# Opening blocks of a two-step top-p attention: the first probe of block 0 (in step 1 also of block 3) moved to VectorE, block 0's mask moved ahead of block 1's probes, and step 1's exponentials put in another order

## The chip, the cores and the metric

The kernel runs on one core of one Trainium2 chip. Times are device microseconds of that core. Most figures are a median of several executions; a figure "in the profile" is from the one execution that the hardware profiler recorded. All executions reported here count as fast ones: on a single core that only means that none lay more than 1.5% above the fastest of the same kernel.

Engines are named as in the profile: PE is TensorE (PEld its loading of weights), DVE is VectorE, ACT is ScalarE, POOL is GpSimd. The granted clock is the share of TensorE's full clock that the profile shows as granted. TensorE is called warm where its operations take their usual time and cold where they take longer: four transposes take 0.60 to 0.66 us warm and some 1.1 us cold in these profiles.

"VectorE's lock" is a name for something that the profiles show of GpSimd. In the first profiles of the two kernels, from 1550 to 3300 us, 232 GpSimd operations started 0.1 us or more after one of VectorE's operations of 4.5 us on 128 x 4096 elements (probes and masks) had started and before it ended: all 232 ended only after it. Where none of these VectorE operations was under way, no GpSimd operation on one column took more than 0.77 us. An operation that ends late in this way is called held.

## The reference, cut to what matters

The program has two layers. The change concerns the second one, which runs two steps of attention over 4096 nodes with the exact top-p ("nucleus") set of each row kept:

```python
def _top_p_attention(X, W1, W2, W3):
    q = X @ W1.T @ W2.T
    k = X @ W3.T
    logits = q @ k.T / TAU
    probs = jax.nn.softmax(logits, axis=-1)
    idx = jnp.argsort(-probs, axis=-1)
    sp = jnp.take_along_axis(probs, idx, axis=-1)
    cs = jnp.cumsum(sp, axis=-1)
    keep_sorted = cs - sp < TOP_P            # 0.9
    ...
    A = probs * mask
    return A / jnp.maximum(A.sum(-1, keepdims=True), 1e-12)

for n in range(STEPS):                       # 2
    A = _top_p_attention(Xa, W1, W2, W3)
    Xf = R @ Xf
    Xa = A @ Xa
    Z = Z + Xf @ U1[n].T + Xa @ U2[n].T
# then X + Z, layer norm over the 256 features
```

## The kernel before

Rows are handled in 32 blocks of 128. Nothing is sorted. For each block the kernel computes the exponentials `e` (128 x 4096, float32), then closes in on the threshold: a "probe" is a sum of all the elements at or below a guess, and some arithmetic on one column turns it into a better guess. After the last probe, what is below the guess is kept in `big`, its largest elements are drawn out ("candidates"), the exact threshold is read off their running sum, and a mask zeroes what is below. TensorE then transposes the masked block and multiplies it with X.

Who does what: TensorE the logits, transposes and products; ScalarE the exponentials, the first probe and the copies out of PSUM; GpSimd the column arithmetic that makes each guess; VectorE the later probes, the candidates and the mask. Step 0 has three probes; step 1, whose first guess is better, skips the second. In the cut below, lines that only allocate or slice are left out.

```python
def exponentials(r, c):                       # 4 of these a block, ScalarE
    nc.scalar.activation(ev[:, :, c, :], r.pm[c], AF.Exp, bias=r.nm, accum_out=...)

def first_probe(r, i):                        # 4 of these a block, ScalarE: sums of Relu and Sign of c1 - e
    nc.scalar.activation(void, r.e[:, ts(h, N // 2)], (AF.Relu, AF.Sign)[i], bias=r.c1, scale=-1.0,
                         accum_out=r.sums[:, h, 2 + i:3 + i])

def lowered(c, y, more):                      # GpSimd: the next guess
    t = col("lowered", 6)
    pool.tensor_tensor(t, inv_e, y, ALU.pow)
    pool.tensor_scalar(t, t, c, more, ALU.mult, ALU.mult)
    return t

def first_step(r):                            # GpSimd, on single columns
    ...                                       # sums, z, L from the four partial sums; r.y1 = fall(r, L)
    if not last:
        r.c2 = lowered(r.c1, r.y1, 1.0)
        pool.tensor_tensor(r.yy, r.y1, r.y1, ALU.mult)
    pool.tensor_tensor(r.up, r.z, mone, ALU.pow)
    pool.tensor_scalar(r.up, r.up, r.sg, ...)
    if last:
        ...
        r.c3 = lowered(r.c1, r.y1, r.up)

def second_probe(r):                          # VectorE, then 17 small operations of GpSimd; step 0 only
    nc.vector.scalar_tensor_tensor(junk, r.e, r.c2, r.e, ALU.is_le, ALU.mult, accum_out=L)
    ...
    r.c3 = lowered(r.c2, y, up)

def third_probe(r):                           # VectorE
    nc.vector.scalar_tensor_tensor(big, r.e, r.c3, r.e, ALU.is_le, ALU.mult, accum_out=r.L)

def masked(r):                                # VectorE
    nc.vector.scalar_tensor_tensor(r.e, r.e, r.t, r.e, ALU.is_ge, ALU.mult, accum_out=kept)

# one step; AHEAD is 4
for b in range(AHEAD):
    ...                                       # 4 x (logits, exponentials) of block b
    for i in range(4):
        first_probe(r, i)
    if b < 2:
        first_step(r)
    if b == 0:
        second_probe(r)
        third_probe(r)
for b in range(NB):
    if b + 1 < NB:
        second_probe(blocks[b + 1])
    candidates(r, found)
    if b + 2 < NB:
        first_step(blocks[b + 2])
    if b + 1 < NB:
        third_probe(blocks[b + 1])
    ...                                       # finishing of earlier blocks
    masked(r)
    attend(r, cur, blocks.get(b - 1), blocks.get(b + AHEAD))
```

`attend` holds TensorE's work on the masked block, and ScalarE's copies, exponentials and first probe of the block four ahead. The program fixes each engine's list, in the order in which it names the operations, and in the profiles the operations behind one that waits come after it. That is why order alone can be worth time here.

Of the kernel before, what the change touches and what calls it, by code (L numbers as in the profile page):

```python
# [20 lines left out]
ALU = mybir.AluOpType  # L21
# [20 lines left out]
AHEAD = 4  # L42
# [5 lines left out]
def gat_then_top_p_diffusion(  # L48
# [562 lines left out]
    def began(n, b, kT, qT, nm, sg, thr, c1):  # L611
        r = SimpleNamespace(n=n, b=b, kT=kT, q=qT[:, ts(b, P)], nm=nm[:, b:b + 1], sg=sg[:, b:b + 1], thr=thr[:, b:b + 1],
                            c1=c1[:, b:b + 1])
        r.e = l1e.tile([P, N], F32, name="e1")
        r.sums = small.tile([P, 2, 4], F32, name="sums", bufs=6)
        return r

    def exponentials(r, c):

        ev = r.e.rearrange("p (h c n) -> p h c n", h=2, c=4)  # L620
        nc.scalar.activation(ev[:, :, c, :], r.pm[c], AF.Exp, bias=r.nm, accum_out=r.sums[:, c // 2, c % 2:c % 2 + 1])  # L621

    def first_probe(r, i):


        h, i = divmod(i, 2)
        void = l1.tile([P, N // 2], I8, name="void")
        nc.scalar.activation(void, r.e[:, ts(h, N // 2)], (AF.Relu, AF.Sign)[i], bias=r.c1, scale=-1.0,  # L628
                             accum_out=r.sums[:, h, 2 + i:3 + i])

    def fall(r, low):

        a, d = col("a"), col("d")
        pool.tensor_scalar(a, r.z, TOP_P - 1.0, low, ALU.mult, ALU.add)
        pool.tensor_scalar(d, r.z, PHI / 0.64, a, ALU.mult, ALU.add)
        pool.tensor_tensor(d, d, mone, ALU.pow)
        pool.tensor_scalar(a, a, d, r.sg, ALU.mult, ALU.mult)
        return a
# [8 lines left out]
    def first_step(r):  # L647
        s, L = r.sums, col("L")
        last = r.n + 1 == STEPS
        r.z, r.yy, r.up = col("z", 6), col("yy"), col("up")  # L650
        pool.tensor_tensor(s[:, 0], s[:, 0], s[:, 1], ALU.add)  # L651
        pool.tensor_scalar(r.z, s[:, 0, 0:1], s[:, 0, 1:2], None, ALU.add)
        pool.tensor_scalar(L, s[:, 0, 3:4], float(N), 0.5, ALU.add, ALU.mult)
        pool.tensor_scalar(L, L, r.c1, s[:, 0, 2:3], ALU.mult, ALU.subtract)
        r.y1 = fall(r, L)
        if not last:
            r.c2 = lowered(r.c1, r.y1, 1.0)
            pool.tensor_tensor(r.yy, r.y1, r.y1, ALU.mult)
        pool.tensor_tensor(r.up, r.z, mone, ALU.pow)
        pool.tensor_scalar(r.up, r.up, r.sg, 0.64 * (11.0 if last else 14.0) / PHI, ALU.mult, ALU.mult)  # L660
        if last:

            pool.tensor_scalar(r.yy, r.y1, -0.2, None, ALU.mult)
            pool.tensor_scalar(r.yy, r.y1, 0.2, r.yy, ALU.mult, ALU.max)
            pool.tensor_scalar(r.yy, r.yy, 1.0, None, ALU.add)
            pool.tensor_scalar(r.up, r.up, r.c1, r.yy, ALU.mult, ALU.add)
            r.c3 = lowered(r.c1, r.y1, r.up)

    def second_probe(r):
        if r.n + 1 == STEPS:  # L670
            return
        L = col("L")
        nc.vector.scalar_tensor_tensor(junk, r.e, r.c2, r.e, ALU.is_le, ALU.mult, accum_out=L)
        rho, y, up = col("rho"), col("y"), col("up2")
        y2 = fall(r, L)

        pool.tensor_scalar(rho, r.y1, y2, r.y1, ALU.subtract, ALU.mult)
        pool.tensor_scalar(rho, rho, 1e-7, None, ALU.max)
        pool.tensor_tensor(rho, rho, mone, ALU.pow)
        pool.tensor_scalar(rho, rho, r.yy, 0.5, ALU.mult, ALU.max)  # L680
        pool.tensor_scalar(rho, rho, 2.0, -1.0, ALU.min, ALU.add)
        pool.tensor_scalar(rho, r.yy, r.thr, rho, ALU.is_gt, ALU.mult)
        pool.tensor_scalar(y, rho, 1.0, y2, ALU.add, ALU.mult)

        pool.tensor_tensor(y2, y, y, ALU.mult)
        pool.tensor_scalar(rho, y2, 3.5, 0.3, ALU.mult, ALU.add)
        pool.tensor_scalar(y2, rho, y2, 1.0, ALU.mult, ALU.add)
        pool.tensor_scalar(up, r.up, r.c2, y2, ALU.mult, ALU.add)
        r.c3 = lowered(r.c2, y, up)

    def third_probe(r):

        r.L = col("L3")
        nc.vector.scalar_tensor_tensor(big, r.e, r.c3, r.e, ALU.is_le, ALU.mult, accum_out=r.L)  # L694

    def candidates(r, found):


        t, after, eighth = (x[:, r.b:r.b + 1] for x in found)
        seg = SEG[r.n + 1 == STEPS]  # L700
        cand = small.tile([P, max(SEG), 8], F32, name="cand", bufs=2)[:, :seg]
        best = small.tile([P, CAND], F32, name="best", bufs=2)

        cum = small.tile([P, CAND + 1], F32, name="cum", bufs=2)
        edges = [N * s // seg for s in range(seg + 1)]
        for s in range(seg):
            nc.vector.max(cand[:, s, :], big[:, edges[s]:edges[s + 1]])  # L707
        nc.vector.tensor_scalar(cum[:, :1], r.z, 1.0 - TOP_P, r.L, ALU.mult, ALU.subtract)
        nc.vector.tensor_reduce(eighth, cand[:, :, 7], AX.X, ALU.max)
        flat = cand.rearrange("p s k -> p (s k)")  # L710
        for i in range(CAND // 8):
            nc.vector.max(best[:, ts(i, 8)], flat)
            if i + 1 < CAND // 8:
                nc.vector.match_replace(flat, best[:, ts(i, 8)], flat, -1.0)
        nc.vector.tensor_tensor_scan(cum[:, 1:], best, zero.to_broadcast([P, CAND]), cum[:, :1], ALU.add, ALU.add)

        drop = small.tile([P, CAND], F32, name="drop", bufs=2)
        work = small.tile([P, CAND], F32, name="work", bufs=2)
        nc.vector.tensor_scalar(drop, cum[:, :CAND], 0.0, 3.0e38, ALU.is_ge, ALU.mult)
        nc.vector.tensor_tensor_reduce(work, drop, best, 1.0, best[:, :1], ALU.add, ALU.min, t)  # L720
        nc.vector.tensor_scalar(work, drop, -1.0, 3.0e38, ALU.mult, ALU.add)
        nc.vector.tensor_tensor_reduce(work, best, work, 1.0, -3.0e38, ALU.subtract, ALU.max, after)
        r.t = t
# [221 lines left out]
    for n in range(STEPS):  # L945
        if n == 0:
            cur = X
        else:
            cur = X
            for g in range(NB // 4):  # L950
                nc.sync.dma_start(cur[:, ts(g, 4), :], xa_d[ts(g, 4)].rearrange("b p d -> p b d"))
        kT, qT, nm, sg, thr, c1 = projections(cur, n)
        found = [table(f"found{i}") for i in range(3)]
        every = {ET.DVE, ET.PE, ET.Activation, ET.Pool}
        blocks = {}
        with tc.manual_schedule(engines=every):
            for b in range(AHEAD):
                r = blocks[b] = began(n, b, kT, qT, nm, sg, thr, c1)
                r.pm = {}
                for c in range(4):  # L960
                    r.pm[c] = logits(r.q, kT, c)
                    exponentials(r, c)
                for i in range(4):
                    first_probe(r, i)
                if b < 2:
                    first_step(r)
                if b == 0:
                    second_probe(r)
                    third_probe(r)
            for b in range(NB):  # L970
                r = blocks[b]
                if b + 1 < NB:
                    second_probe(blocks[b + 1])
                candidates(r, found)
                if b > 2:
                    finish_scale(blocks[b - 3])
                if b + 2 < NB:
                    first_step(blocks[b + 2])
                if b + 1 < NB:
                    third_probe(blocks[b + 1])  # L980
                if b > 1:
                    finish(blocks[b - 2])
                if b > 2:
                    finish_rows(blocks.pop(b - 3))
                masked(r)
                if b + AHEAD < NB:
                    blocks[b + AHEAD] = began(n, b + AHEAD, kT, qT, nm, sg, thr, c1)
                attend(r, cur, blocks.get(b - 1), blocks.get(b + AHEAD))
            r = blocks[NB - 1]
            finish(blocks[NB - 2])  # L990
            contributed(r, contribute(r))
            finish(r)
            for b in range(NB - 3, NB):
                finish_scale(blocks[b])
            for b in range(NB - 3, NB):
                finish_rows(blocks[b])
        repaired(n, kT, qT, nm, cur, found)
# [32 lines left out]
```

## Time and profile before

| | before |
|---|---|
| median of three executions | 3413.57 us (3408.16 to 3417.34) |
| span in the profile | 3405.8 us, granted clock 0.945 |
| first exponential of step 0 to the start of its last mask | 805.99 us |
| first exponential of step 1 to the end of the program | 901.48 us |
| in step 1: first exponential to TensorE's first product | 59.88 us |
| in step 1: one block on TensorE | 24.33 us |

The page's first line of figures gives the busy time of each engine in us, its share of the span and the count of its instructions:

```profile
PE 3023.5 (89%) x19243; PEld 2431.8 (71%) x19243; DVE 2616.3 (77%) x5070; ACT 2009.1 (59%) x3182; POOL 1160.3 (34%) x1804
```

These shares average over stages that are limited by different engines, so they say little on a change at two openings.

To compare executions I set the clock of each step to zero at that step's first exponential. What lies before it (the first layer, projections, the reload of X between the steps) differs by some microseconds from execution to execution and has nothing to do with the change: the first exponential of step 0 came at 1553.8 to 1565.0 us over all profiles of this study.

### The profile page before, as it was taken

How to read it: one execution, taken by the hardware profiler on the slowest of the kernel's cores; microseconds unless marked ns; L12 is line 12 of the kernel's file. 1: busy time of each engine (PE TensorE's matmuls, PEld its weight loads, DVE VectorE, ACT ScalarE, POOL GpSimd, SP SyncE). 2: the span in 40 equal slices, each digit the busy share in tenths (PEclk: the TensorE clock that was granted, in tenths of full speed). 3: DMA queues.
4: the chain of work that ended last, by engine and by line, in shares of the span. 5: the costliest groups of instructions: out<-in, count | busy, mean ns of one | idle time of the engine just before them, and what ended most of it. 6: DMA issues, size and time to landing. Idle time of an engine off the chain costs nothing. (4 is left out here: it accounts for less than half of the span.)

```text
span 3405.8 us, 52192 instructions
## 1 busy us (share of the span) xinstructions
PE 3023.5 (89%) x19243; PEld 2431.8 (71%) x19243; DVE 2616.3 (77%) x5070; ACT 2009.1 (59%) x3182; POOL 1160.3 (34%) x1804
## 2 busy tenths in 40 slices
PE   4499898898989999983999999999849999999994
PEld 3399798897968888751777777777526777777783
DVE  6589898999966555414999999997148888888864
ACT  4588787886841100046676767672367777777731
POOL 3100201102010000006776767672034656565620
PEclk7699999999999999986999999999869999999997
DMA  9726548383155555400000000000100000000000
GB/s 262 209 89 171 172 118 244 106 215 128 44 169 172 163 171 167 131 11 1 13 16 18 16 18 17 18 16 18 61 1 10 24 21 24 21 24 21 24 19 11
DMA packets 198827, 268.62 MB, mean 79 GB/s; under 512 B 14240, under 2 KB 156064, under 8 KB 198560
## 3 DMA queue, kind: packets, MB, share of 16 engines
q1 hardware_dynamic: 152272, 207.99, 18.8%
q0 software_dynamic: 16896, 33.56, 5.4%
q10 hardware_dynamic: 29392, 23.60, 2.2%
q8 instruction: 157, 2.57, 0.3%
q14 instruction: 110, 0.90, 0.1%
HBM read 226.89 MB, written 71.76 MB: 88 GB/s over the span
## 5 line engine op out<-in xcount | busy, mean ns | idle before, releaser
L800 PE MATMUL acc<-X,eT 128*128 128x256 f32 x4160 | 977.1, 381 | 8.3 <-ACT eT L794 8.3
L800 PEld LDWEIGHTS acc<-X,eT 128*128 128x128 f32 x4160 | 763.8, 191 | 95.4 <-ACT eT L794 8.8
L284 PE MATMUL acc<-ut,m 128*128 128x195 bf16 (+1 forms) x8192 | 730.3, 249 | 85.5 <-DVE m L272 49.4
L284 PEld LDWEIGHTS <-m 128*128 128x128 bf16 x8192 | 702.4, 98 | 113.4 <-DVE m L272 66.4
L265 ACT ACTIVATE g<-sr,d_big 128x1024 bf16<-128x1024 f32 x512 | 550.6, 1180 | 49.8 <-DVE m L271 39.8
L628 ACT ACTIVATE void<-e,c 128x2048 int8<-128x2048 f32 x256 | 514.6, 2010 | 1.0
L621 ACT ACTIVATE e<-mm,nm 128x1024 f32<-128x1024 f32 x256 | 286.0, 1117 | 341.9 <-PE mm L483 341.8
L425 PE MATMUL racc<-hl,ar 128*128 128x512 f32 x2048 | 470.5, 392 | 14.8 <-issue 10.4
L425 PEld LDWEIGHTS racc<-hl,ar 128*128 128x128 f32 x2048 | 385.8, 189 | 99.3 <-issue 11.3
L794 ACT COPY eT<-tp 128x512 f32<-128x512 f32 x520 | 303.8, 584 | 171.8 <-PE tp L792 171.8
L792 PEld LDWEIGHTS tp<-ident,e 128*128 128x128 f32 x2080 | 246.2, 142 | 212.8 <-issue 95.5
L792 PE MATMUL tp<-ident,e 128*128 128x128 f32 x2080 | 325.2, 280 | 51.4 <-DVE e L773 29.9
L483 PE MATMUL mm<-kT,qT 64*128 64x512 f32 x1024 | 303.8, 679 | 61.6 <-ACT e L621 50.9
L271 DVE TENSOR_TENSOR m<-g,ax 128x2048 bf16<-128x2048 bf16 x256 | 313.1, 1223 | 41.7 <-ACT g L265 38.7
L707 DVE MAX8 cand<-big 128x8 f32<-128x228 f32 (+1 forms) x1088 | 343.8, 394 | 0.0
L272 DVE TENSOR_TENSOR m<-ax,m 128x2048 bf16<-128x2048 bf16 x256 | 315.9, 1234 | 26.2 <-PE acc L284 0.5
L694 DVE SCALAR_TENSOR_TENSOR big<-e,lowered 128x4096 f32<-128x4096 f32 x64 | 286.8, 4481 | 34.0 <-POOL lowered L644 34.0
L421 DVE CAST ar<-at 128x1024 fp32r<-128x1024 bf16 x256 | 177.1, 692 | 169.5 <-PE racc L425 166.5
L728 DVE SCALAR_TENSOR_TENSOR e<-e,found 128x4096 f32<-128x4096 f32 x64 | 287.6, 4494 | 0.0
L436 ACT ACTIVATE xf<-xf,rinv 128x256 f32<-128x256 f32 x64 | 32.6, 510 | 372.3 <-DVE xf L435 370.0
L651 POOL TENSOR_TENSOR sums<-sums 128x4 f32<-128x4 f32 x64 | 116.7, 1823 | 301.9 <-ACT void L628 301.9
L483 PEld LDWEIGHTS mm<-kT,qT 64*128 64x128 f32 x1024 | 84.0, 197 | 159.3 <-issue 80.2
(239 smaller groups left out, 3242.8 us busy)
## 6 DMA issues: line engine op xcount, KB each, us to landing
at<-adj_d SPq DMA_DIRECT2D x256, 256.0 KB, 3.1
ut<-uv_d SPq DMA_DIRECT2D x60, 784.0 KB, 4.5
ax<-in_adj_t_dram POOLq DMA_DIRECT2D x32, 1024.0 KB, 13.6
adj_d<-ax SPq DMA_DIRECT2D x32, 1024.0 KB, 11.2
uv_d<-parts ACTq DMA_DIRECT2D x32, 392.0 KB, 8.4
xf<-xf_d SPq DMA_DIRECT2D x65, 128.0 KB, 2.0
sr<-s_d SPq DMA_DIRECT2D x16, 512.0 KB, 4.2
xf_d<-xf ACTq DMA_DIRECT2D x64, 128.0 KB, 2.4
```

The costliest lines, as they stand in the source:

```text
L265: nc.scalar.activation(g[:, c, :], shared[k].sr, AF.Relu, scale=BIG, bias=d_big[:, h, j:j + 1])
L271: nc.vector.tensor_tensor(m[0], g, a, ALU.min)
L272: nc.vector.tensor_tensor(m[1], a, m[0], ALU.subtract)
L284: nc.tensor.matmul(shared[k].acc[i][:, t, :cols], m[t][:, c, ts(i, P)], shared[k].ut[j // QUARTER][:, j % QUARTER, t, :cols], start=(j == ...
L425: nc.tensor.matmul(acc[i].rearrange("p s d -> p (s d)"), ar[:, c, ts(i, P)], hl[hop][:, j].rearrange("p s d -> p (s d)"), start=(j == 0), ...
L483: nc.tensor.matmul(pm[:, h, :], q[ts(h, DA), :], kT[ts(h, DA), ts(c, 512)], start=True, stop=True)
L628: nc.scalar.activation(void, r.e[:, ts(h, N // 2)], (AF.Relu, AF.Sign)[i], bias=r.c1, scale=-1.0, accum_out=r.sums[:, h, 2 + i:3 + i])
L707: nc.vector.max(cand[:, s, :], big[:, edges[s]:edges[s + 1]])
L728: nc.vector.scalar_tensor_tensor(r.e, r.e, r.t, r.e, ALU.is_ge, ALU.mult, accum_out=kept)
L792: nc.tensor.transpose(pt[:, i, :], r.e[:, ts(4 * g + i, P)], ident)
L794: nc.scalar.copy(eT, pt)
L800: nc.tensor.matmul(r.acc[:, 0, :], eT[:, i, :], cur[:, j, :], start=(j == 0), stop=(j == NB - 1))
```

## The change

The intent: at the start of a step ScalarE has a queue of exponentials and first probes of four blocks, while VectorE and TensorE wait. So the first probe of block 0, in step 1 also that of block 3, becomes one VectorE operation; block 0 gets its mask before VectorE turns to block 1; and in step 1 ScalarE does the exponentials of blocks 0 and 1 together, then a probe, then those of 2 and 3 together, then a probe.

```diff
+    def direct_probe(r):
+        r.low = col("low")
+        nc.vector.scalar_tensor_tensor(junk, r.e, r.c1, r.e, ALU.is_le, ALU.mult, accum_out=r.low)
 ...
     def first_step(r):
 ...
+        direct = hasattr(r, "low")
+        used = 2 if direct else 4
 ...
+        if direct:
+            L = r.low
+        else:
             (the two operations that make L from ScalarE's sums)
 ...
-            for b in range(AHEAD):
-                (exponentials of b; first probe of b; first_step for b < 2;
-                 second and third probe for b == 0)
+            filled(0)
+            direct_probe(blocks[0])
+            first_step(blocks[0])
+            second_probe(blocks[0])
+            third_probe(blocks[0])
+            filled(1)
+            probed(1)
+            first_step(blocks[1])
+            filled(2)
+            if last:
+                filled(3)
+                probed(2)
+            else:
+                probed(2)
+                filled(3)
+                probed(3)
             for b in range(NB):
                 r = blocks[b]
-                if b + 1 < NB:
+                if 0 < b < NB - 1:
                     second_probe(blocks[b + 1])
                 candidates(r, found)
+                if b == 0:
+                    masked(r)
 ...
                 if b + 2 < NB:
                     first_step(blocks[b + 2])
+                if b == 0:
+                    second_probe(blocks[1])
                 if b + 1 < NB:
                     third_probe(blocks[b + 1])
+                if b == 0 and last:
+                    direct_probe(blocks[3])
 ...
-                masked(r)
+                if b > 0:
+                    masked(r)
```

`filled(b)` is the four pairs of logits and exponentials of block b, `probed(b)` its first probe on ScalarE. In step 0 the order of ScalarE's queue stays: only block 0's probe is gone from it.

More of the change, by code (lines that the diff above doesn't have):

```diff
@@ L650, in first_step @@
         r.z, r.yy, r.up = col("z", 6), col("yy"), col("up")
-        pool.tensor_tensor(s[:, 0], s[:, 0], s[:, 1], ALU.add)
+        direct = hasattr(r, "low")
+        used = 2 if direct else 4
+        pool.tensor_tensor(s[:, 0, :used], s[:, 0, :used], s[:, 1, :used], ALU.add)
         pool.tensor_scalar(r.z, s[:, 0, 0:1], s[:, 0, 1:2], None, ALU.add)
-        pool.tensor_scalar(L, s[:, 0, 3:4], float(N), 0.5, ALU.add, ALU.mult)
-        pool.tensor_scalar(L, L, r.c1, s[:, 0, 2:3], ALU.mult, ALU.subtract)
+        if direct:
+            L = r.low
+        else:
+            pool.tensor_scalar(L, s[:, 0, 3:4], float(N), 0.5, ALU.add, ALU.mult)
+            pool.tensor_scalar(L, L, r.c1, s[:, 0, 2:3], ALU.mult, ALU.subtract)
         r.y1 = fall(r, L)
@@ L956, in gat_then_top_p_diffusion, with filled @@
         with tc.manual_schedule(engines=every):
-            for b in range(AHEAD):
-                r = blocks[b] = began(n, b, kT, qT, nm, sg, thr, c1)
+            last = n + 1 == STEPS
+            def filled(b):
+                r = blocks[b]
                 r.pm = {}
@@ L962, in gat_then_top_p_diffusion, with probed @@
                     exponentials(r, c)
+            def probed(b):
                 for i in range(4):
-                    first_probe(r, i)
-                if b < 2:
-                    first_step(r)
-                if b == 0:
-                    second_probe(r)
-                    third_probe(r)
+                    first_probe(blocks[b], i)
+            for b in range(AHEAD):
+                blocks[b] = began(n, b, kT, qT, nm, sg, thr, c1)
+            filled(0)
[14 more added lines that the diff above has]
+                probed(3)
             for b in range(NB):
                 r = blocks[b]
-                if b + 1 < NB:
+                if 0 < b < NB - 1:
                     second_probe(blocks[b + 1])
                 candidates(r, found)
+                if b == 0:
+                    masked(r)
                 if b > 2:
```

## The prediction

> **What bounds the kernel now.** The change touches only the opening of the two attention steps, so I first looked for where those openings lie. I read, in this order, the page's slices (attention runs from slice 18 to the end), a table of 25 us stretches over both steps, and then, engine by engine, the order of instructions around the two openings and the two ends. There is one core, granted clock 0.945, and all runs count as fast. The stretches of step 0, then of step 1 (busy us of PE, PEld, DVE, ACT, POOL, then the granted clock):
>
> ```profile
> 1555.00:1580.00 25.00, 11.60 (x38) 3.24 (x34) 4.49 (x2) 23.05 (x29) 9.92 (x17) 0.84 0.00 0
> 1605.00:1630.00 25.00, 12.23 (x46) 7.58 (x47) 24.34 (x53) 13.09 (x18) 22.28 (x34) 0.66 0.00 1
> 1630.00:1655.00 25.00, 25.00 (x129) 18.86 (x128) 24.34 (x53) 18.25 (x29) 22.29 (x33) 1.00 0.03 11
> ...
> 2305.00:2330.00 25.00, 20.80 (x105) 18.04 (x104) 24.45 (x52) 5.74 (x10) 17.93 (x31) 0.93 0.05 17
> ```
>
> ```profile
> 2505.00:2530.00 25.00, 12.55 (x36) 3.86 (x32) 4.74 (x3) 22.18 (x29) 5.26 (x16) 0.70 0.00 1
> ...
> 2655.00:2680.00 25.00, 25.00 (x131) 18.91 (x130) 22.14 (x58) 18.24 (x27) 14.88 (x19) 1.00 0.08 23
> ```
>
> The reader is to see three regimes. Each opening belongs to ScalarE (ACT), with PE and VectorE (DVE) mostly idle. In the middle of step 0, PE and DVE are both full: a block takes 24.33 us on PE and 24.36 us on DVE. Towards its end PE drops to 20.80 of 25 while DVE stays full, so step 0 ends when DVE lets it. In step 1 only PE is full (24.33 us a block against DVE's 22.1 of 25), so step 1 ends when PE lets it.
>
> Step 0's opening on DVE (L673 is the second probe, L694 the third, L707 starts the candidates, L728 is the mask), and PE's first transposes and one near the end of the step:
>
> ```profile
> 1572.97 4.49 DVE L673 SCALAR_TENSOR_TENSOR junk<-e,lowered 128x4096 uint8<-128x4096 f32 x1 [23.12 <-POOL lowered L644]
> 1585.45 4.49 DVE L694 SCALAR_TENSOR_TENSOR big<-e,lowered 128x4096 f32<-128x4096 f32 x1 [7.99 <-POOL lowered L644]
> 1593.72 4.53 DVE L673 SCALAR_TENSOR_TENSOR junk<-e,lowered 128x4096 uint8<-128x4096 f32 x1 [3.77 <-POOL lowered L644]
> 1598.18 5.31 DVE L707 MAX8 cand<-big 128x8 f32<-128x256 f32 x16
> ...
> 1608.81 4.48 DVE L694 SCALAR_TENSOR_TENSOR big<-e,lowered 128x4096 f32<-128x4096 f32 x1
> ...
> 1613.22 4.48 DVE L728 SCALAR_TENSOR_TENSOR e<-e,found 128x4096 f32<-128x4096 f32 x1
> ```
>
> ```profile
> 1617.77 1.12 PE L792 MATMUL tp<-ident,e 128*128 128x128 f32 x4 [13.65 <-DVE e L728]
> ...
> 2324.16 1.94 PE L792 MATMUL tp<-ident,e 128*128 128x128 f32 x8 [3.85 <-DVE e L728]
> ```
>
> Step 1's opening: the last of 16 first probes on ACT, and PE's first product, which waits for a copy queued behind it:
>
> ```profile
> 2562.40 0.19 ACT L628 ACTIVATION_READ_ACCUMULATOR void<-e,c 128x1 f32 x1
> ```
>
> ```profile
> 2564.20 3.78 PE L800 MATMUL acc<-X,eT 128*128 128x256 f32 x8 [8.29 <-ACT eT L794]
> ```
>
> The two openings are therefore held by different things: DVE's chain in step 0, ACT's queue in step 1.
>
> [...] GpSimd's power on one column takes 0.55 us alone and 4.82 us when it meets the probe at 1572.97. [...] four transposes take 1.12 us at 1617.77 and 0.66 us later.
>
> **The change part by part.** A first probe of one block on ACT is four passes, 1560.16 to 1568.63 in step 0, so 8.4 us with the accumulator reads. The same sum on DVE is one operation of 4.49 us. Blocks 0 of both steps, and block 3 of step 1, move to DVE. The mask of block 0 moves ahead of block 1's second and third probes.
>
> Step 0 on DVE. The exponentials of block 0 end at 1560.12 as before. The direct probe runs from 1560.2 to 1564.7. GpSimd's sum z is held by the lock to about 1564.9; from its next operation to the lowered threshold took 2.76 us (1570.17 to 1572.93), so the second probe starts at 1567.7 instead of 1572.97. From it to the third probe took 12.48 us, GpSimd's arithmetic in between; third probe at 1580.2. It then needs 4.5, the candidates 10.6 (1598.18 to 1608.81), and the mask starts at 1595.4 and ends at 1600.0 instead of 1617.7. PE may start 17.7 us sooner.
>
> But that is not the gain. Block 1's probes used to sandwich block 0's candidates, which hid GpSimd's arithmetic between them (1598.49 to 1605.56, 7.07 us). Now the second probe of block 1 runs from 1600.05 to 1604.5 and its third directly follows, so DVE idles some 7.2 us. The third probe starts at 1611.7, later than the 1608.81 of before. After it, the mask of block 0 no longer follows: before, the second probe of block 2 came at 1617.82; now at 1611.7 + 4.4 = 1616.1. From there DVE's sequence is the old one, without a gap. So DVE is ahead by 1.7 us, and the mask of block 1 ends at 1640.0 instead of 1641.7. PE, early with block 0, waits for it. As DVE sets the end of step 0, step 0 gains 1.7 us. The check by sum: initial wait and probes save 5.2, the wait at 1593.72 saves 3.8, the new gap costs 7.2; total 1.8.
>
> Step 1 on ACT. It runs exponentials of 0 and 1, probe 1, exponentials of 2 and 3, probe 2: two probes of 8.4 fewer ahead of PE's first copy, 16.8 us. Exponentials of block 3 now directly follow those of block 2, without a probe in which PE fills two banks ahead. At PE's cold pace the exponentials come 1.7 us apart (2504.32 to 2506.02), warm 1.2, against some 6.2 us for a block before; I take -0.5 to +1 us. ACT is then free at about 2545.7 instead of 2562.5, and PE's first product starts about 16.8 us sooner, near 2547.4.
>
> Does DVE keep up? Direct probe to 2514.7, GpSimd's chain 5.05 us (2520.14 to 2525.19) to 2520.0, third probe of 0 to 2524.5, candidates 10.9 to 2535.4, mask to 2540.0: before ACT is ready, so not on the path. Then third probe of 1, direct probe of 3 (4.45 each), candidates 10.9, third probe of 2 and mask of 1 (4.45 each) end at 2568.7. PE, 21.7 us with block 0 as before (2564.20 to 2585.90) and 1.55 us of other work first, wants it at 2570.7. A slack of 2 us; later masks have more. GpSimd's step for block 2 is stretched by the probe of block 3 to about 2555, needed at 2559.8. So PE keeps nearly the whole 16.8 us to the end, where it is still the bound.
>
> Sum: 1.7 + 16.8 = 18.5 us, 0.54% of 3413.57.
>
> **The rivals.** First: both openings gain what the mask of block 0 gains, 17 to 18 us each, 35 us together, 3379 us. For it: PE starts by that much earlier in both. Against it: DVE has no idle time in step 0 after 1598 and PE waits for it at the end. Second: in step 1, masks and GpSimd's lock take the place of ACT's queue, because DVE carries three more operations of 4.49 us in the opening; if the mask of block 1 comes 5 us late, 13 us remain in all, 3400 us. For it: only 2 us of slack. Third: nothing is won, or time is lost, because the new gap in step 0 is longer than 7.2 us (GpSimd held by locks) or PE cools twice. A cold start costs about 2.5 us on PE, but DVE's pace covers it at the end of step 0: 3396 to 3399 us. Fourth: the threshold from the direct sum differs in the last digits and a block more has to be repaired. The repair of one block lasts some 70 us, from 3334 to the end of the trace. The one there now has ties, and its search for a threshold did not run, so it depends on data and should stay alone.
>
> **Range and chances.** I predict 3395 us. The three runs before lie 9 us apart, so the median may be off by 5; the mechanism adds 4 on either side. Range 3386 to 3404. Faster by 2% would need 68 us, more than both openings hold idle; slower by 2% only a repair more.
>
> **What would show it.** In step 0, the mask of block 0 near 1600, a DVE gap of about 7 us ended by GpSimd's lowered threshold before block 1's third probe, and PE waiting for the mask of block 1 near 1640. The last mask of step 0 should be only 1 to 3 us earlier. In step 1, PE's first product should come 16 to 18 us sooner relative to the first exponential, and no wait for a mask after it. A step 0 shorter by over 8 us, or a wait for masks in step 1, would prove me wrong.

## The result, and the profile after

| | before | changed |
|---|---|---|
| median of four executions, same rounds | 3412.61 us | 3392.55 us (3388.07 to 3393.72) |
| ratio, 95% interval | | 0.9939 (0.9921 to 0.9956) |
| span in the profile | 3405.8 us | 3391.9 us |
| first exponential of step 0 to the start of its last mask | 805.99 us | 808.38 us |
| first exponential of step 1 to the end | 901.48 us | 885.33 us |
| in step 1: to TensorE's first product | 59.88 us | 40.19 us |

A ratio here is the mean time of one kernel's fast executions over that of the other's in the same rounds, so it isn't quite the ratio of the medians beside it. By it the changed kernel is within 2% of the one before, 0.6% faster, and 3392.55 lies 2.5 us from the 3395.0 predicted. Yet two rows do not fit the argument. Step 0, said to gain 1.7 us, is 2.4 us longer in the profile; and TensorE's first product is 19.7 us sooner, not 16.8, of which only 16.2 us arrive at the end.

First what went as said. VectorE in step 0's opening, changed kernel (start, duration, engine, line, operation, then the idle time before it and what ended it; L634 is the direct probe, L683 the second, L704 the third, L738 the mask):

```profile
1560.03 4.51 DVE L634 SCALAR_TENSOR_TENSOR junk<-e,c 128x4096 uint8<-128x4096 f32 x1 [10.22 <-ACT e L621]
1567.62 4.48 DVE L683 SCALAR_TENSOR_TENSOR junk<-e,lowered 128x4096 uint8<-128x4096 f32 x1 [3.06 <-POOL lowered L649]
1580.12 4.49 DVE L704 SCALAR_TENSOR_TENSOR big<-e,lowered 128x4096 f32<-128x4096 f32 x1 [8.01 <-POOL lowered L649]
...
1595.28 4.48 DVE L738 SCALAR_TENSOR_TENSOR e<-e,found 128x4096 f32<-128x4096 f32 x1
...
1599.88 4.49 DVE L683 SCALAR_TENSOR_TENSOR junk<-e,lowered 128x4096 uint8<-128x4096 f32 x1
1611.62 4.48 DVE L704 SCALAR_TENSOR_TENSOR big<-e,lowered 128x4096 f32<-128x4096 f32 x1 [7.25 <-POOL lowered L649]
1616.04 4.48 DVE L683 SCALAR_TENSOR_TENSOR junk<-e,lowered 128x4096 uint8<-128x4096 f32 x1
```

Every one of these is within 0.2 us of the prediction's time for it, the new gap of 7.25 us included. TensorE starts 18 us sooner and then waits for the mask of block 1 (second line), and still waits for masks at the end of the step (last line):

```profile
1599.83 1.12 PE L802 MATMUL tp<-ident,e 128*128 128x128 f32 x4 [5.74 <-DVE e L738]
...
1640.11 1.09 PE L802 MATMUL tp<-ident,e 128*128 128x128 f32 x4 [14.95 <-DVE e L738]
...
2326.36 1.94 PE L802 MATMUL tp<-ident,e 128*128 128x128 f32 x8 [4.18 <-DVE e L738]
```

Now step 1. ScalarE's last read of a first probe's accumulator comes at 2544.95, 38.4 us after the step's first exponential at 2506.57 (before: 2562.40, 58.1 us after 2504.32), and TensorE follows:

```profile
2544.95 0.19 ACT L628 ACTIVATION_READ_ACCUMULATOR void<-e,c 128x1 f32 x1
```

```profile
2546.76 1.99 PE L810 MATMUL acc<-X,eT 128*128 128x256 f32 x8 [0.87 <-ACT eT L804]
...
2566.89 0.44 PE L823 MATMUL tp<-ident,xf 128*128 128x128 f32 x2
...
2570.62 1.09 PE L802 MATMUL tp<-ident,e 128*128 128x128 f32 x4 [3.08 <-DVE e L738]
2571.64 2.08 PE L483 MATMUL mm<-kT,qT 64*128 64x512 f32 x4
2573.65 1.11 PE L802 MATMUL tp<-ident,e 128*128 128x128 f32 x4
2574.56 2.79 PE L830 MATMUL acc<-u,eT 128*128 128x256 f32 x8
```

The third line has a wait of 3.08 us for the mask of block 1, which the prediction had said would not be there. VectorE on the way to that mask (third probe of block 1, direct probe of block 3, third probe of block 2, mask of block 1):

```profile
2541.87 4.49 DVE L704 SCALAR_TENSOR_TENSOR big<-e,lowered 128x4096 f32<-128x4096 f32 x1
...
2546.28 4.48 DVE L634 SCALAR_TENSOR_TENSOR junk<-e,c 128x4096 uint8<-128x4096 f32 x1
...
2561.59 4.48 DVE L704 SCALAR_TENSOR_TENSOR big<-e,lowered 128x4096 f32<-128x4096 f32 x1
...
2565.99 4.48 DVE L738 SCALAR_TENSOR_TENSOR e<-e,found 128x4096 f32<-128x4096 f32 x1
```

What follows the wait on TensorE runs slow: four logits take 2.08 us where they took 1.13 before the wait, four transposes 1.09 to 1.11 where 0.6 is usual. The granted clock was 1.00 before the wait (2563.0 to 2567.5 us) and 0.50 after it (2570.6 to 2576.0 us).

The same line of the page for the changed kernel, and a warning about it:

```profile
PE 3022.0 (89%) x19243; PEld 2431.0 (72%) x19243; DVE 2629.2 (78%) x5076; ACT 1984.9 (59%) x3158; POOL 1274.7 (38%) x1798
```

ScalarE has 24 instructions fewer (three first probes, each four passes with a read of the accumulator) and VectorE 6 more, as written (three direct probes, each with a read). GpSimd has 6 fewer, yet is busy for 114 us more. The stretch from 2005 to 2030 us of step 0, where nothing was changed, has it too (busy us of PE, PEld, DVE, ACT, POOL, then granted clock, DMA share and GB/s). Before:

```profile
2005.00:2030.00 25.00, 25.00 (x129) 18.86 (x128) 24.45 (x50) 18.24 (x27) 18.01 (x31) 1.00 0.05 16
```

Changed:

```profile
2005.00:2030.00 25.00, 25.00 (x128) 18.73 (x127) 24.45 (x50) 18.20 (x27) 22.49 (x31) 1.00 0.07 22
```

The same 31 instructions take GpSimd 4.5 us more of 25. So the open questions were: is step 0's extra length a consequence of the change, and what does each opening really bring?

### The profile page after: what moved, and what is told of

It reads as the page before. It is cut to its first block, busy times and chain, and to the rows that moved or that the text cites. A ratio compares the mean times of both kernels' runs of the same rounds, so it can differ in the third digit from the quotient of the medians.

```text
span 3391.9 us, 52166 instructions
## 1 busy us (share of the span) xinstructions
PE 3022.0 (89%) x19243; PEld 2431.0 (72%) x19243; DVE 2629.2 (78%) x5076; ACT 1984.9 (59%) x3158; POOL 1274.7 (38%) x1798
## 3 DMA queue, kind: packets, MB, share of 16 engines
q1 hardware_dynamic: 152272, 207.99, 18.4%
## 5 line engine op out<-in xcount | busy, mean ns | idle before, releaser
L628 ACT ACTIVATE void<-e,c 128x2048 int8<-128x2048 f32 x244 | 490.5, 2010 | 0.6
L425 PEld LDWEIGHTS racc<-hl,ar 128*128 128x128 f32 x2048 | 386.2, 189 | 99.4 <-issue 10.2
L704 DVE SCALAR_TENSOR_TENSOR big<-e,lowered 128x4096 f32<-128x4096 f32 x64 | 286.8, 4480 | 20.6 <-POOL lowered L649 20.6
L738 DVE SCALAR_TENSOR_TENSOR e<-e,found 128x4096 f32<-128x4096 f32 x64 | 288.1, 4502 | 0.0
L658 POOL TENSOR_TENSOR sums<-sums 128x4 f32<-128x4 f32 (+1 forms) x64 | 100.9, 1577 | 262.4 <-ACT void L628 234.5
```

The lines of the kernel that those rows point to most:

```text
L425: nc.tensor.matmul(acc[i].rearrange("p s d -> p (s d)"), ar[:, c, ts(i, P)], hl[hop][:, j].rearrange("p s d -> p (s d)"), start=(j == 0), ...
```

## The experiments

After the run that answered the prediction, eleven more were made, in three groups, each group on one chip. All outputs are right.

### The two kernels again, and each opening alone

Two theories of step 0. P: the new order of the opening locks GpSimd and VectorE into a worse phase for the rest of the step, and costs what the profile showed. R: step 0 has two paces, and chance picks one in each execution, whatever the kernel. Two theories of the sum: both openings gain 17 us, or only step 1's does. The same two kernels ran again, beside two hybrids that have the old order in one of the steps:

```diff
+            old = last            # step0_only; step1_only has: old = not last
             filled(0)
-            direct_probe(blocks[0])
+            if old:
+                probed(0)
+            else:
+                direct_probe(blocks[0])
 ...
-            if last:
+            if last and not old:
 ...                               (and likewise at each place of the loop)
```

> The kernel before, unchanged, as a second profile and a measure of the noise. Theory P (phase): the first profile of before had VectorE at 24.36 us a block in the middle of step 0 and GpSimd busy 18.0 of 25 us; the changed kernel 24.42 us (five blocks 25.05) and GpSimd 22.5 of 25, because GpSimd's short operations meet three locked VectorE operations a block instead of two. If the phase belongs to the order of instructions, this profile repeats 24.36 and 18.0. Theory R (run to run): the phase is chance, and this profile may show 24.42 and 22.5; then step 0 lasts some 2 to 4 us longer than in the first profile and the time nears the upper runs of before (3412 to 3417). Ratio to before 1.000 within 0.15% in both.

> The changed kernel, unchanged, again. Theory P: step 0's blocks again at 24.42 us or more, last mask of step 0 about 2 us later after the first exponential than in the first profile of before. Theory R: in this profile they may be at 24.36 and the last mask 1.7 us earlier. Both: step 1, from first exponential to the end, 885 us against 901.5; time 18 to 21 us below before.

> The new opening in step 0 alone, step 1 in the old order. Prediction's step: 1.7 us faster than before. Theory P: 0 to 3 us slower, since the lead of 1.7 us at the mask of block 1 is lost to the slower phase of GpSimd. Rival 'both openings gain what the mask of block 0 gains': 17 us faster, 3396.

> The new opening in step 1 alone, step 0 in the old order. Prediction's step: 16.8 us faster. My reading of the two traces: 16.3 us faster, made of 22.3 us won until PE has done block 0 and 6.0 us given back while PE waits cold for the mask of block 1; PE's wait for that mask 3.1 us as in the changed kernel. Rival: only half of the gain is step 1's, so 9 us.

| kernel | median, us | before, same rounds | ratio (95%) | step 0: to last mask | step 1: to first product | step 1: to the end |
|---|---|---|---|---|---|---|
| before_again | 3408.65 | 3409.47 | 0.9994 (0.9982 to 1.0007) | 812.26 | 59.54 | 901.24 |
| after_again | 3386.20 | 3409.47 | 0.9933 (0.9918 to 0.9948) | 809.54 | 40.31 | 883.70 |
| step0_only | 3408.50 | 3409.47 | 0.9996 (0.9983 to 1.0009) | 809.31 | 58.93 | 900.33 |
| step1_only | 3391.74 | 3409.47 | 0.9954 (0.9941 to 0.9967) | 810.47 | 39.69 | 883.19 |

The new opening of step 0 alone is worth nothing that can be measured; that of step 1 alone is worth 0.46%, 15.7 us of 3409. The rival by which both openings gain 17 us is gone. (The two add up to 17.1 us, where both together, in after_again, gave 22.8 us; each figure has an interval of 4 to 5 us to either side.)

And theory P is in trouble: the unchanged kernel, run again, took 812.26 us to its last mask, longer than the changed kernel in any of its profiles. The stretch that had differed, in before_again:

```profile
2005.00:2030.00 25.00, 24.43 (x126) 18.13 (x125) 24.45 (x50) 17.69 (x27) 22.49 (x31) 1.00 0.05 17
```

GpSimd's 22.49 is that of the changed kernel's first profile, with the old order. Whether the changed kernel could also have the shorter pace was still open; the next runs showed it.

### Step 1: which mask is late, and what removes the wait

The theory by now: in step 1 TensorE arrived at block 1 some 5 us sooner than I had reckoned, and found the mask of block 1 unfinished, because VectorE puts the direct probe of block 3 (4.5 us) and two third probes ahead of it. Then a kernel with that probe behind the mask ("late3") has no wait and keeps all of the lead. The other question is what the move of block 3's probe brings net, since a part of what ScalarE saves is lost in that wait: "act3" puts it back on ScalarE. A third kernel ("fill") goes at the gap of 7.25 us in step 0's opening, by putting the second probe of block 1 ahead of block 0's candidates. The fourth has late3 and fill together.

act3:

```diff
             if last:
                 filled(3)
                 probed(2)
+                probed(3)
 ...
-                if b == 0 and last:
-                    direct_probe(blocks[3])
```

late3:

```diff
-                if b + 2 < NB:
+                if b + 2 < NB and not (last and b == 1):
                     first_step(blocks[b + 2])
 ...
-                if b == 0 and last:
-                    direct_probe(blocks[3])
 ...
                 if b > 0:
                     masked(r)
+                if b == 1 and last:
+                    direct_probe(blocks[3])
+                    first_step(blocks[3])
```

fill:

```diff
             first_step(blocks[1])
+            second_probe(blocks[1])
             filled(2)
 ...
-                if b == 0:
-                    second_probe(blocks[1])
```

> Changed kernel, but block 3 of step 1 probed on ScalarE again (block 0 stays on VectorE). Prediction's step (ScalarE's queue sets the opening, VectorE keeps up): PE's first product 8.4 us later and all of it kept, so 8.4 us slower than the changed kernel. My reading of the traces (PE was stopped by the late mask of block 1 anyway): the first product comes 8.4 us later, at about 48.6 us after the first exponential, but PE no longer waits for the mask of block 1 (3.1 us) and doesn't cool (2.9 us), so only 2 to 3 us slower than the changed kernel; step 1 about 887 us.

> Changed kernel with the direct probe of block 3 in step 1 moved behind the mask of block 1. My reading: the mask of block 1 starts 55.0 instead of 59.4 to 60.0 us after step 1's first exponential, PE doesn't wait for it, block 1 takes PE 24.4 instead of 30.3 us, step 1 is 5 to 6 us shorter (878 to 879 us from first exponential to end). Prediction's step (slack of 2 us at that mask): no change.

> Changed kernel with block 1's second probe in step 0 ahead of block 0's candidates, so that GpSimd's arithmetic for block 1 lies under the candidates. Prediction's step (a gap of 7.2 us before block 1's third probe eats the early mask): the gap goes, a wait of 3.6 us for block 1's first threshold takes its place, the mask of block 1 starts about 76.9 us after the first exponential instead of 80.4 to 80.7, and step 0 is 3.5 us shorter, give or take 3 us for GpSimd's phase. Rival (the phase of GpSimd takes it all): same step 0 as the changed kernel.

> Both of the last two together: their gains add, 8 to 10 us faster than the changed kernel, 25 to 33 us faster than before.

| kernel | median, us (before: 3411.31) | ratio (95%) | step 0: to block 1's mask / to last mask | step 1: to first product | block 1 on TensorE | step 1: to the end |
|---|---|---|---|---|---|---|
| act3 | 3393.25 | 0.9950 (0.9935 to 0.9965) | 80.53 / 804.43 | 48.62 | 24.33 | 889.76 |
| late3 | 3388.38 | 0.9931 (0.9918 to 0.9945) | 80.36 / 804.31 | 40.06 | 24.32 | 880.33 |
| fill | 3387.62 | 0.9934 (0.9920 to 0.9948) | 77.88 / 803.83 | 39.78 | 27.67 | 883.26 |
| fill_late3 | 3386.46 | 0.9923 (0.9908 to 0.9938) | 78.30 / 802.25 | 39.90 | 24.33 | 880.05 |

**late3** does what the theory says. TensorE's transposes of `xf`, one pair at the start of each block from block 1 on, in late3:

```profile
2565.96 0.44 PE L823 MATMUL tp<-ident,xf 128*128 128x128 f32 x2
...
2590.28 0.44 PE L823 MATMUL tp<-ident,xf 128*128 128x128 f32 x2
```

They are 24.32 us apart: block 1 takes as long as any other. In the changed kernel's profile the same two were 30.3 us apart. The mask of block 1 in late3, and TensorE's first transposes of that block, now without a wait:

```profile
2560.78 4.48 DVE L738 SCALAR_TENSOR_TENSOR e<-e,found 128x4096 f32<-128x4096 f32 x1
```

```profile
2566.45 0.60 PE L802 MATMUL tp<-ident,e 128*128 128x128 f32 x4
```

The mask starts 55.0 us after the first exponential, as expected (59.4 in the changed kernel). Step 1 ends at 880.33 us, 2.9 to 5.0 us sooner than in the profiles with the changed opening. I had expected 878 to 879. TensorE lost nothing in the blocks between: from the transposes of block 1 to those of the last block late3 takes the same time as before, to 0.1 us. But from there to the same transposes in the repair of one block at the end it takes 71.0 us, against 69.6 in the first profile of before. This stretch varied from 69.6 to 71.0 us over all profiles, so differences of about 1 us in the last column are noise. The timed executions don't separate late3 from the changed kernel (0.9931 beside 0.9933 to 0.9943, each with an interval of 0.13 to 0.18% to either side); what it gains is read from the profiles.

The cause of the late mask is shown; the cost varied. In after_again the wait was shorter:

```profile
2576.23 0.63 PE L802 MATMUL tp<-ident,e 128*128 128x128 f32 x4 [1.26 <-DVE e L738]
2576.79 1.13 PE L483 MATMUL mm<-kT,qT 64*128 64x512 f32 x4
```

Transposes of 0.63 and logits of 1.13 us are warm, and block 1 took 25.77 us there. TensorE itself had come 2.4 us later: it had begun block 0 cold (its first eight products took 3.78 us). In step1_only and fill the wait was 3.19 and 3.15 us, yet the transposes and logits after it were warm (0.63 and 1.13 us), and block 1 took 27.7 us. So the missed mask gave back 1.4 to 6.0 us within block 1, depending on the wait and on whether TensorE was cold after it. The length of the wait alone doesn't decide that (it was cold after 3.08 us, not after 3.19); what does, no run here shows.

**act3** separates two things that the change had joined. Its first product comes 8.4 us later than the changed kernel's, the size of one first probe on ScalarE, exactly as the prediction priced it. But its block 1 doesn't wait, so at the end only 4.4 to 6.6 us are lost against the changed kernel (889.76 against 883.2 to 885.3 over six profiles). I had expected a loss of 2 to 3 us; so more of block 3's move reaches the end than I thought, and less than the 8.4 us that the prediction priced. Part of the miss: in act3 TensorE began block 0 cold (3.40 us for the first eight products, not 1.99), which cost 1.4 us. Against late3, where no wait hides it, act3 ends 9.4 us later: the probe's 8.4 us and this, within the noise of the repair. The timed runs agree in sign, but the intervals overlap: 0.9950 beside 0.9939, 0.9933 and 0.9943 for the changed kernel in other rounds.

**fill** brings forward the mask of block 1 in step 0 by 2.5 us, a part of the gap of 7.25 us. I had put it at 76.9 us, a microsecond too early. I had counted on the first of these two waits (as 3.6 us), not on the second:

```profile
1589.11 4.48 DVE L683 SCALAR_TENSOR_TENSOR junk<-e,lowered 128x4096 uint8<-128x4096 f32 x1 [3.78 <-POOL lowered L649]
...
1614.01 4.48 DVE L683 SCALAR_TENSOR_TENSOR junk<-e,lowered 128x4096 uint8<-128x4096 f32 x1 [0.81 <-POOL lowered L649]
```

The first wait is for the guess of block 1, whose first probe is only then finished on ScalarE. The gap is not a matter of order alone: the old order had a wait of 3.77 us at just this place. At the last mask only some 0.5 us of the 2.5 are left (803.83 beside 804.3 to 804.4): this step ran its first eight blocks in the longer pace described below and the rest in the shorter one. fill_late3, in the shorter pace throughout, kept 2.1 us (802.25). The timed runs don't separate fill (0.9934) from the changed kernel either.

These four also ended theory P. In act3 and late3, which have exactly the changed kernel's step 0, the last mask comes at 804.43 and 804.31 us: 1.6 us ahead of the 805.99 of the first profile of before. So the changed order has the short pace too, and in it the lead of block 1's mask (82.07 to 80.4 us) is all there 30 blocks later.

### What the two paces are

In the short pace a block takes VectorE 24.36 us and in the long one 24.42, with single blocks of 25.06; over step 0 they differ by 3 to 6 us for the same order. What differs is which of GpSimd's small operations run into VectorE's lock, and how many: from each mask to the next, blocks 3 to 29, two are held in the first profile of before (short pace) and three in the changed kernel's (long pace). The power takes 0.55 us alone and 4.82 us when held. One operation can be held by two in a row: the multiplication L649, 0.34 us otherwise in step 1, took 8.33 us from 2562.19 in the changed kernel, through a third probe (from 2561.59) and the mask that followed (from 2565.99). GpSimd's chain to the second guess in the profile of before (short pace); L659 makes `up`, L634 is the first operation that needs the second probe's sum:

```profile
2036.33 0.26 POOL L634 TENSOR_SCALAR a<-z,L 128x1 f32<-128x1 f32 x1 [4.58 <-DVE junk L673]
...
2047.37 4.01 POOL L644 TENSOR_SCALAR lowered<-lowered,c 128x1 f32<-128x1 f32 x1
...
2051.49 0.54 POOL L659 TENSOR_TENSOR up<-z,mone 128x1 f32<-128x1 f32 x1
2052.14 3.98 POOL L660 TENSOR_SCALAR up<-up,sg 128x1 f32<-128x1 f32 x1
```

The same part of the changed kernel's first profile (long pace), where the lines are L669 for `up` and L639 for the first operation that needs the sum:

```profile
2029.35 3.94 POOL L649 TENSOR_SCALAR lowered<-lowered,c 128x1 f32<-128x1 f32 x1
2033.24 0.19 POOL L668 TENSOR_TENSOR yy<-a 128x1 f32<-128x1 f32 x1
2033.39 4.82 POOL L669 TENSOR_TENSOR up<-z,mone 128x1 f32<-128x1 f32 x1
2038.31 0.26 POOL L670 TENSOR_SCALAR up<-up,sg 128x1 f32<-128x1 f32 x1
2038.68 0.27 POOL L639 TENSOR_SCALAR a<-z,L 128x1 f32<-128x1 f32 x1
```

In the short pace the mask holds only the last operation of `up` (L660, 3.98 us), when the guess is long ready, and GpSimd idles 4.58 us until the probe's sum is there. In the long pace GpSimd is three operations behind: the mask holds the multiplication that makes the guess (L649, 3.94 us), which ends just before VectorE's second probe starts with that guess at 2033.31. `up` starts just after this probe, is shown as "busy" for 4.82 us while it waits for the lock, and then L670 and the chain follow late, at 2038.68. GpSimd has no reserve left: the guess is there 0.03 us before that probe starts. When the mask catches the operation before that multiplication, the power L648, VectorE has to wait for the guess. GpSimd in another block of the same profile:

```profile
1781.96 4.85 POOL L648 TENSOR_TENSOR lowered<-inv_e,a 128x1 f32<-128x1 f32 x1
1786.92 0.26 POOL L649 TENSOR_SCALAR lowered<-lowered,c 128x1 f32<-128x1 f32 x1
```

and VectorE there:

```profile
1781.92 4.47 DVE L738 SCALAR_TENSOR_TENSOR e<-e,found 128x4096 f32<-128x4096 f32 x1
1787.21 4.49 DVE L683 SCALAR_TENSOR_TENSOR junk<-e,lowered 128x4096 uint8<-128x4096 f32 x1 [0.61 <-POOL lowered L649]
```

The power at 1781.96 starts 0.04 us behind the mask, loses 4.3 us, and VectorE then idles 0.61 us for its result. The traces bear this out without exception. In blocks 3 to 29 of step 0 in the twelve profiles without spare operations, a block took 24.34 to 24.38 us where its mask held the last operation of `up` (157 blocks), 24.41 to 24.45 where it held the multiplication (143), and 25.04 to 25.12 where it held the power (24). By this reading GpSimd, 34% busy on the page but 18.01 to 22.49 of 25 us in the middle of step 0, is close to binding that step. That can be tested by giving it a little more to do: four spare operations in each block's first step.

```diff
         pool.tensor_scalar(r.up, r.up, r.sg, 0.64 * (11.0 if last else 14.0) / PHI, ALU.mult, ALU.mult)
+        if not last:
+            for i in range(4):
+                pool.tensor_scalar(col("spare"), r.up, r.sg, None, ALU.mult)
```

With it ran the changed kernel a third time and the best kernel a second time.

> Changed kernel with four spare one-column GpSimd multiplications at the end of each block's first step in step 0 (their results are read by nobody; about 1.4 us of GpSimd time a block). Eight profiles of full blocks in step 0 fall into two paces, 24.36 us a block (GpSimd's threshold for the next block is ready in time) and 24.42 with single blocks of 25.06 (it is ready just at or 0.6 us after the end of the mask). Theory P (GpSimd's unlocked time is what separates the two paces): with more of it the fast pace is out of reach, no block at 24.36, VectorE waits for GpSimd's threshold, and the last mask of step 0 starts 809 us or more after the first exponential, instead of 804.4 in the fast pace. Rival (GpSimd is idle 2.5 to 7 of 25 us, so nothing of it matters): paces as before, 24.36 or 24.42 by chance, last mask at 804 to 809.5 us.

> The changed kernel a third time, for a profile of its phase beside the next run on one chip. From first exponential to end of step 1 883.2 to 885.3 us; PE's block 1 in step 1 between 25.8 and 30.3 us; ratio to before 0.992 to 0.995.

> The combined version again, beside the changed kernel on one chip: step 0's last mask 2 us earlier than the changed kernel's in the fast pace (802.3 against 804.4), step 1 from first exponential to end 880.0 to 880.5 us; 4 to 8 us faster than the changed kernel.

| kernel | median, us (before: 3414.09) | ratio (95%) | step 0: to last mask | VectorE, us a block in step 0 | step 1: to the end |
|---|---|---|---|---|---|
| more_pool | 3449.70 | 1.0101 (1.0086 to 1.0116) | 856.94 | 26.18 | 885.27 |
| after_third | 3394.05 | 0.9943 (0.9930 to 0.9956) | 804.28 | 24.36 | 885.28 |
| fill_late3_b | 3390.23 | 0.9926 (0.9913 to 0.9939) | 805.56 | 24.42 | 880.07 |

The four operations show 1.06 us of busy time in a block. They cost 1.8 us in each block of step 0 and 55.7 us in all by the medians (52.7 us to the last mask), because VectorE now waits for GpSimd's guess: in blocks 3 to 29 each mask holds an operation with three more to do before the guess. The size was not foreseen: theory P said only 809 us or more for the last mask. The second probes of two successive blocks in more_pool, 26.18 us apart:

```profile
1782.80 4.49 DVE L686 SCALAR_TENSOR_TENSOR junk<-e,lowered 128x4096 uint8<-128x4096 f32 x1 [1.71 <-POOL lowered L649]
...
1808.98 4.49 DVE L686 SCALAR_TENSOR_TENSOR junk<-e,lowered 128x4096 uint8<-128x4096 f32 x1 [1.71 <-POOL lowered L649]
```

So GpSimd's unlocked time is a bound of step 0, only just hidden in the kernel before and in the changed one. after_third fell in the short pace and fill_late3_b in the long one, with orders that had been seen in the other pace: chance picks it, and R stands for these kernels, with the correction from fill that the pace can also change within a step. What sets the phase in one execution is not known, and timed executions without a profile don't show which pace they had, so how much of any median is pace stays open. The changed kernel's executions spread over 3381.84 to 3398.80 us in one group, more than the two paces explain.

The kernel with the lowest ratios is fill_late3: 0.9923 and 0.9926 of the kernel before, in two groups. Against the changed kernel in the same group that is 0.9926 over 0.9943, 0.17% or some 6 us, where I had expected 4 to 8 (8 to 10 in the first of the two groups). The two intervals overlap, so the timed runs alone don't show this gain; in the profiles step 1 is 5.2 us shorter (885.28 to 880.07 us). A like kernel that saves GpSimd an operation, by making `up` in one instruction, did not build.

## Why the prediction was right or wrong

The total was right: 3392.55, 3386.20 and 3394.05 us in three groups, all a little below 3395.0 and in the range (the second by a hair). Its steps:

- **Step 0's opening, time by time: right.** The second and third probes, mask 0 and the gap of block 1 came within 0.2 us, and TensorE then waited at 1640 as said.
- **"Step 0 gains 1.7 us": right, where it can be compared.** In the short pace the last mask moved from 805.99 us (one profile) to 804.28, 804.31 and 804.43. The long pace agrees in sign: 812.26 and 810.47 in the old order, 808.38, 809.54 and 809.31 in the new. The step that the text lacked is that step 0 has two paces, 3 to 6 us apart: the prediction took VectorE's sequence after the opening as fixed. Read alone, the first pair of profiles says the opposite of the truth, a step 0 that got 2.4 us slower.
- **"16.8 us sooner" for TensorE's first product in step 1: too small.** It was 19.7 us (59.88 to 40.19), outside the 16 to 18 us that it named as a sign. The term that was mis-sized is that of the exponentials, "-0.5 to +1 us"; it was 2.9. In pairs they took less: from the first exponential, blocks 0 and 1 needed 10.2 us and the four blocks 21.7 us in all, where before they took 24.6 (each counted up to ScalarE's next operation). With no probe between them, ScalarE waits for logits 0.13 us twice in block 1, where before it waited 1.08 and 0.50 us in that block, after a probe in which TensorE had idled (8.47 us).
- **"TensorE 21.7 us with block 0 as before": wrong by 2.6 us.** It took 19.1 us, since it came warm: the first eight products took 1.99 us at a granted clock of 1.00, not 3.78 at 0.50. The prediction had taken the cold start over from the old trace. It does not always go: in after_again they took 3.78 us again, and block 0 21.4.
- **"A slack of 2 us" for the mask of block 1: wrong, and the real miss.** The mask itself came as said (its end 63.9 us after the first exponential; the prediction's 2568.7 makes 64.4). TensorE wanted it 5.5 us sooner than reckoned, by the two points above (2.9 + 2.6). The slack of 2 became a wait of 3.08 us. I had checked whether VectorE could keep up with a TensorE that was as slow as before, not with the one that the change would make.
- **"TensorE keeps nearly the whole 16.8 us": right in size, by two errors that cancel.** In the first profile TensorE stood 22.3 us ahead at the start of block 1 (82.64 to 60.32 us), then lost 6.0 us in it (24.33 to 30.32), and 16.2 us reached the end. Over six profiles with this opening step 1 took 884.3 us in the mean, against 901.0 in three with the old one: 16.7 us.
- **The sum.** 1.7 from step 0 in like paces and 16.7 from step 1 make 18.4 us. The three groups' ratios, mean 0.9938, are 21.1 us of 3413. The 2.7 us between lie within the intervals (each some 5 us to either side), and no run explains them.
- **The rivals.** Both openings gaining 17 us: refuted by step0_only. The mask of block 1 late: it was, and that rival had the right place; it took TensorE's arrival from the old pace as I did, hence 13 us in its sum for both steps rather than 18.4 to 21.1. The gap longer than 7.2 us: no, 7.25. TensorE cold twice in step 0: it was (transposes of 1.12 us at 1599.83 and of 1.09 at 1640.11, both at a granted clock of 0.50), and VectorE's pace covered it, as that rival itself allowed; in step 1 it was cold once more, after the wait. The 2.5 us that the rival gave a cold start compare with 2.3 and 2.6 us in block 0 of step 1 (21.4 and 21.7 us cold, 19.1 warm). A further repair: no; from the repair's test for ties (2.35 us on VectorE, at 3349.99 and 3336.01) to the end of the trace it is 55.8 us before and 55.9 after.
- **Its own test.** It named "a wait for masks in step 1" as what would prove it wrong. That wait was there, so by its own words the mechanism of step 1 was not the one described, though the number was right.

## What to carry to other kernels

When a change lets one engine start sooner, check each buffer it will want against the time at which the engine will then arrive, at its new speed (here 19.1 us for block 0), not at the pace of the old trace (21.7). An engine whose busy time is in large part waiting can be close to the bound while its share, averaged over a whole program, looks small (here GpSimd: 34% on the page, 18.01 to 22.49 of 25 us in the middle of step 0, and four operations of 1.06 us cost 1.8 us a block); adding a known, tiny load to it, and seeing whether the step gets longer by more than that, is a cheap test. And before a difference of a few microseconds in one stage is put down to a change, run the unchanged kernel again with a profile: here the same kernel differed from itself by more than the change did in step 0.
